# A transformer block on one core: Vector work spread over the beats of a unit, part of it given to GpSimd in another order

## The chip, the cores and the metric

The kernel runs on one core of one Trainium2 chip, in float32, with some matmul operands split into a high and a low part. The metric is the time of one execution in device microseconds (us). Engines are named as in the profile: PE is TensorE (PEld its weight loads), DVE is VectorE ("Vector"), ACT is ScalarE, POOL is GpSimd, SP is the queue that issues nearly all DMAs.

## The reference

A diffusion-transformer block over 16 samples of 256 tokens by 256 channels, 16 heads of 16 channels, with a context of 256 tokens per sample and a condition vector per sample:

```python
shift_a, scale_a, gate_a, shift_m, scale_m, gate_m = split(silu(c) @ W_mod + b_mod, 6)
q, k, v = split((ln(x) * (1 + scale_a) + shift_a) @ W_qkv + b_qkv, 3)       # per head
x = x + gate_a * (softmax(q @ k.T * scale) @ v @ W_proj + b_proj)            # self attention
q_c = ln(x) @ W_qc + b_qc;  k_c, v_c = split(ln(context) @ W_kvc + b_kvc, 2)
x = x + softmax(q_c @ k_c.T * scale) @ v_c @ W_cproj + b_cproj               # cross attention
h = gelu((ln(x) * (1 + scale_m) + shift_m) @ W_mlp1 + b_mlp1)
x = x + gate_m * (h @ W_mlp2 + b_mlp2)                                       # MLP
```

## The kernel before

**Units and beats.** The work is cut into 32 *units*, each the attention of one sample: an s unit is self attention, a c unit cross attention. The order (from line 709) is s0 to s4, then s5, c0, s6, c1 and so on to s15, c10, then c11 to c15. So units 5 to 25 alternate, odd ones s and even ones c, and from unit 26 on all are c. In the loop of line 1123 each unit passes through eight *beats*, `beat(n, k)` (line 981). A beat of unit n does a bit of several units at once: scores of unit n+1, exponentials and value products of unit n, projections and transposes of units n+2 and n+3, layer norms of n+3 and n+4, and the output projection and additions of n-1 to n-3. After the last unit the MLP follows, four chunks per sample.

**Order.** Every engine's instructions run in the order in which the Python code issues them (`InOrder`, line 41): what one waits for holds all behind it on its engine. SP's DMAs stand in one queue of this kind too.

**One beat.** `visit` (line 966) opens it. Four matmuls write scores of unit n+1 into the two PSUM banks `s` (`s_tile`, line 628), and one Vector reduction takes their maxima, `mx`. There is only one such pair of banks, so the next beat's s must wait for this beat's mx. Then four matmuls write the transposed scores of unit n into the pair of banks `st` (`t_part`, line 664), and one ACT activation takes the exponential into `pt` (`exp`); the next st waits for it. After that, even and odd beats differ:

- Even beats do the value products `o` (`av_part`, line 694, 16 matmuls) of one quarter of the heads. In beats 0 and 4 the maxima of half the heads are first transposed (`m_part`, line 656, tile `psm`), scaled by ACT to `m` and sent by DMA into a row of the next q.
- Odd beats run the *lanes* (lines 402 to 431): twelve pairs of 64-row matmuls, each pair for two projections, one with either half of the array. In beat 1 Q with V, in 3 the output projection P with Q, in 5 K with P, in 7 V with K. The first two thirds of a lane read the high part of the input (`xTh`), the last third the low part (`xTl`).

**What the other engines do beside it, before the change.** A projection's K and Q come from PSUM as a high part (ACT, `h_...`) and a low part (DVE, `l_...`, beats 0 and 4) and go by DMA into the stacked tiles `big` for the scores. Layer norms (`layernorm`, line 294): statistics `st` and aggregates `mv` on DVE, an add of epsilon on DVE and a power of -0.5 on POOL for `rs`, then the application `xn` on POOL. Names end with the input: `_s` (x of an s unit), `_c` (context), `_q` (x after self attention, for a c unit), `_m` (MLP). The normed input is transposed on PE into PSUM (`transposed`, line 332, tile `psT`); of an s unit ACT makes the high part and DVE the low part, from the bank; of a c unit ACT makes a high part and a full copy `y` (one buffer), and POOL the low part from these. After attention (`build_post`, line 543) the values `oT` are copied out of PSUM by ACT, pulled by DMA into `U` and, for the denominators, `S`; DVE takes reciprocals of S; these go through DRAM and come back spread as `R`; POOL multiplies U by R; DVE casts U to the high part `xTh_a`, POOL subtracts for the low part `xTl_a`; then come the projection P, and the additions `t`, `x` and the gate `xg` on POOL.

**Where these steps stand in a unit before the change.** Beat 0: transposes of unit n+3, additions of n-3, U of n-2. Beat 1: ACT's high part of the transposes, `xTh_a` (DVE) and `xTl_a` (POOL) of n-2, and the whole layer norm c of unit n+4 (its statistics, aggregates and epsilon on DVE, the rest on POOL). Beat 2: low part or full copy of the transposes; gate. Beat 3: reciprocal. Beat 4: transposes of `xn_q`, copy `oT`, and for an s unit n+4 its statistics, aggregates and epsilon. Beat 5: application of that norm, pull of the first half of oT, R's DMA, statistics of `_q`. Beat 6: full copy `y_q` (ACT), low part `xTl_q` (POOL), then aggregates and epsilon (DVE), power and application (POOL) of `_q`.

**Banks.** PSUM tiles of the short tag `tr` (two banks, `ps_gen`, line 68) hold in turn `psm`, `psT` and `o`; a bank is free again when the last reader of its tile is done. The long tag `gen` (two banks) holds the lanes' results.

Of the kernel before, what the change touches and what calls it, by code (L numbers as in the profile page):

```python
# [21 lines left out]
def pixart_block(  # L22
# [32 lines left out]
    E_ = {'M': ((-17, -12, -10, -1, 1), (0, 3, 4, 7, 9), (8, 11, 13, 15)), 'LN': {'s': 'pool', 'c': 'pool', 'q': 'pool'}, 'ON': (1, 1, 1), 'H': (7, 11, 14, 15), 'AP': 23, 'DV': (0, 1), 'HP': (1, 0), 'W1P': [(-9, 1), (-8, 1), (-7, 1), (-6, 1), (-5, 1), (-5, 5), (-4, 1), (-4, 3), (-4, 5), (-3, 1), (-3, 3), (-3, 5), (-2, 1)], 'W2P': [(-4, 7), (-3, 0), (-3, 4), (-3, 6), (-3, 7), (-2, 2), (-2, 4), (-2, 6), (-1, 0), (-1, 1)], 'PRE': 'z0qp z0kp load rest ld2 one0 silu b12 brow L0a turn L0b b4 L0d scale T0t sc1 hik lok T0h T0l b4 shift b4 hiq L1a L1b bk loq K0a K0b K0x K0yp L1d T1t K0l T1h K0s Q0a Q0m bq Q0h Q0x Q0yp T1l Q0l Q0s z1kp z1qp K1a K1b hiv lov Q1a Q1b K1x K1y K1l K1s Q1x Q1y Q1l Q1s L2a L2b L2c V0a V0b bv b5 ld3', 'SL': {(-1, 0): 'V1a', (-1, 1): 'T2t T2h T2p vone z2kp z2qp', (-1, 2): 'V1b', (-1, 3): 'rest', (-1,4): 'M0 rest one1 ld4', (-1, 5): 'K2a L3a', (-1, 6): 'K2m L3b L3p L3c', (-1, 7): 'd3 one2 rest', (0, 0): 'd6 rest', (0, 1): 'rest', (0, 2): 'd3', (0, 4): 'rest', (1, 0): 'rest', (1, 2): 'rest', (1, 4): 'rest', (30, 0): 'd3', (30, 1): 'd2', (30, 2): 'd3', (30, 5): 'd3', (31, 1): 'd2'}}  # L55
# [45 lines left out]
    def load_x(b):  # L101
        X[b] = work.tile([P, NT, H], F32, tag="x", name=f"x_{b}", bufs=5)
        SP.dma_start(X[b], tok(x, b))
# [84 lines left out]
    def f_load():  # L188
        X[0] = work.tile([P, NT, H], F32, tag="x", name="x_0", bufs=5)
# [104 lines left out]
    def layernorm(src, name):  # L294
# [34 lines left out]
        o.steps, o.pow = [stats, rstd, apply], pow  # L329
# [213 lines left out]
    def build_post(u):  # L543
# [150 lines left out]
    def av_part(u, g):  # L694
# [33 lines left out]
    def mlp_load(b):  # L728
        m = M[b] = Box()
        m.h, m.hT = {}, {}  # L730
        m.xt = work.tile([P, NT, H], F32, tag="x", name=f"x2_{b}", bufs=5)
# [94 lines left out]
    def mlp_w1():  # L826
# [3 lines left out]
        for j in range(4):  # L830
            wf.append(stage(W_mlp1, j * H, f"w1_{j}", "x"))
            yield
# [30 lines left out]
    def mlp_w2():  # L863

        wf = []
        for j in range(4):
            wf.append(work.tile([P, 2, H], F32, tag="x", name=f"w2_{j}", bufs=5))
# [113 lines left out]
    def beat(n, k):  # L981
# [12 lines left out]
        early = lc if lc and lc.b not in (0, B - 1) else None  # L994
        if k == 0 and q2:
# [13 lines left out]
        if k == 0:  # L1009
# [5 lines left out]
            if q3:  # L1015
                q3.T[0].turn()
# [3 lines left out]
            if p3:  # L1020
                p3.add()
            if p2:
                p2.norm()
            if ls and n > 0:
                load(ls)
        elif k == 1:
# [4 lines left out]
            if q3:  # L1031
                q3.T[0].high()
            if p2:
                p2.high()
                p2.low()
            if lc:
                lc.ln[0].steps[0]()
                lc.ln[0].steps[1]()
                lc.ln[0].steps[2]()
        elif k == 2:  # L1040
# [3 lines left out]
            if q3 and q3.kind == "s":  # L1044
                q3.T[0].low()
            elif q3:
                q3.T[0].full()
                q3.T[0].rest_pool()
            if late:
                for f in lx.ln[1].steps:  # L1050
                    f()
            if p1:
                p1.gate()
        elif k == 3:
# [8 lines left out]
            if prev:  # L1063
                p1.recip()
                p1.spread()
        elif k == 4:
# [152 lines left out]
```

## Time and profile before

| | |
|---|---|
| three runs | 810.2, 810.96 and 813.42 us; median 810.96 |
| the profiled execution | 812.03 us, of which the span from first to last instruction is 810.2 |
| granted TensorE clock, mean | 0.982 |
| unit 0 begins its exponentials at | 39.61 us of the span |
| the last of 256 exponentials | unit 31, which begins at 588.19 |
| MLP after the units | to 810.2 us |

A row of the view in order of time gives start, duration, engine, line, operation, output<-inputs with shapes, and in brackets the idle time of the engine before it and what ended it. All instructions have line 51, because a helper issues them; they are told apart by tiles. Merged rows (x2, x4) span from the first start to the last end, and an engine may begin its next instruction some 0.1 us before the end that is written. Rows of groups give count, busy us and mean ns of one, then idle time before them.

### The profile page before, as it was taken

The page shows a single profiled execution, that of the slowest core. Times are in us where ns is not written, and L with a number is a line of the kernel's source. Part 1 is how long each engine was busy: PE and PEld are TensorE (multiplying, and loading weights), DVE is VectorE, ACT ScalarE, POOL GpSimd, SP SyncE. Part 2 cuts the span into 40 slices and gives each one's busy share as a digit, 9 for nine tenths or more (in the row PEclk, how much of TensorE's full clock was granted, in tenths as well). Part 3 has the DMA queues.
Part 4 walks back from the last instruction along what each step waited for, and adds up shares of the span by engine and source line. Part 5 has one row for each costly group of instructions (what it writes and reads, how often), then busy time and mean ns, then how long its engine had stood idle before and what let it go on. Part 6 is the DMA issues. An engine that isn't in the chain of part 4 may idle for free.

```text
span 810.2 us, 22526 instructions
## 1 busy us (share of the span) xinstructions
PE 749.7 (93%) x9071; PEld 616.3 (76%) x9071; DVE 585.7 (72%) x983; ACT 545.3 (67%) x961; POOL 506.1 (62%) x435
## 2 busy tenths in 40 slices
PE   9899889999999999999999787899898899999997
PEld 8677767777777777777777666667568899999997
DVE  4868877878888788887888676777772466566562
ACT  3367767777787877878777666677546466665663
POOL 5754585677656767567676767654546666566563
PEclk9999999999999999999999998999999999999999
DMA  5445334443534545445444434434422222212312
GB/s 193 153 158 187 134 133 154 155 164 137 180 137 164 179 155 167 148 162 180 150 162 165 138 133 157 133 134 168 135 79 73 63 61 78 79 41 78 77 37 58
DMA packets 77165, 106.15 MB, mean 131 GB/s; under 512 B 12355, under 2 KB 40293, under 8 KB 77061
## 3 DMA queue, kind: packets, MB, share of 16 engines
q1 hardware_dynamic: 76084, 103.92, 38.8%
q8 instruction: 71, 1.16, 0.6%
q0 software_dynamic: 160, 0.52, 0.2%
q10 hardware_dynamic: 816, 0.27, 0.1%
q14 instruction: 34, 0.27, 0.1%
HBM read 35.89 MB, written 8.98 MB: 55 GB/s over the span
## 4 chain that ended last, share of the span: by engine, by line
PE 41%; DVE 25%; POOL 18%; issue 9%; ACT 5%; DMA 1%; SPq 0%; POOLq 0%; ACTq 0%; DVEq 0%
DVE mx L51 11%; PE s L51 11%; PE st L51 5%; DVE xn_m L51 5%; PE o L51 5%; POOL x L51 3%; POOL hl L51 3%; PE ps_q L51 3%; PE ph L51 2%; POOL xn_q L51 2%; PE ps_P_c L51 2%; PE ps_k L51 2%; PE ps_P_s L51 2%; PE ps_v_s L51 2%; PE ps_v_c L51 2%
## 5 line engine op out<-in xcount | busy, mean ns | idle before, releaser
L51 DVE TENSOR_REDUCE mx<-s 128x4 f32<-128x1024 f32 x252 | 307.9, 1222 | 97.1 <-PE s L51 95.2
L51 ACT ACTIVATE pt<-st 128x1024 f32<-128x1024 f32 x256 | 261.4, 1021 | 111.6 <-PE st L51 109.9
L51 PE MATMUL s<-big 63*128 63x256 f32 x1008 | 121.8, 314 | 41.4 <-DVE mx L51 38.0
L51 PEld LDWEIGHTS s<-big 63*128 63x128 f32 x1008 | 79.8, 188 | 90.3 <-DVE mx L51 80.7
L51 PE MATMUL o<-pt,v 128*32 128x256 f32 x2048 | 138.0, 387 | 0.0
L51 POOL TENSOR_TENSOR hl<-hf,hh 128x512 fp32r<-128x512 f32 x64 | 89.3, 1405 | 57.6 <-ACT hh L51 47.9
L51 PE MATMUL st<-big 64*128 64x256 f32 (+1 forms) x1040 | 111.3, 287 | 1.7 <-ACT pt L51 1.7
L51 PEld LDWEIGHTS st<-big 64*128 64x128 f32 (+1 forms) x1040 | 84.3, 189 | 6.2 <-ACT pt L51 3.1
L51 PEld LDWEIGHTS o<-pt,v 128*32 128x32 f32 x2048 | 53.7, 109 | 39.0 <-issue 1.3
L51 ACT ACTIVATE hf<-ph,bT 128x256 f32<-128x256 f32 x120 | 50.3, 472 | 28.9 <-PE ph L51 28.9
L51 ACT ACTIVATE hh<-ph,bT 128x256 fp32r<-128x256 f32 x120 | 50.4, 471 | 25.0 <-PE s L51 14.2
L51 PE MATMUL ph<-wkch,wself 128*128 128x256 f32 x256 | 52.8, 289 | 0.0
L51 PE MATMUL ph<-wqch,wself 128*128 128x256 f32 x256 | 51.7, 285 | 0.0
L51 DVE TENSOR_SCALAR xn_m<-x,mv_m,rs_m 128x256 f32<-128x256 f32 x32 | 38.8, 1251 | 10.9 <-POOL rs_m L51 10.9
L51 PE MATMUL s<-big,hh 128*128 128x256 f32 x256 | 46.3, 280 | 0.1
L51 PE MATMUL st<-big,hh 128*128 128x256 f32 x256 | 45.5, 278 | 0.0
L51 POOL TENSOR_TENSOR rs_s<-rs_s,mhalf 128x2 f32<-128x2 f32 x16 | 11.4, 712 | 52.1 <-DVE rs_s L51 50.5
L51 PEld LDWEIGHTS ph<-wkch,wself 128*128 128x128 f32 x256 | 42.7, 195 | 0.3
L51 POOL TENSOR_TENSOR rs_q<-rs_q,mhalf 128x2 f32<-128x2 f32 x16 | 11.4, 712 | 49.4 <-DVE rs_q L51 49.2
L51 PEld LDWEIGHTS ph<-wqch,wself 128*128 128x128 f32 x256 | 42.0, 191 | 0.4 <-DVE hk L51 0.4
L51 POOL TENSOR_TENSOR xTl_q<-y_q,xTh_q 128x512 fp32r<-128x512 f32 x16 | 20.7, 1292 | 34.0 <-ACT y_q L51 28.8
L51 POOL TENSOR_SCALAR xn_c<-c,mv_c,rs_c 128x256 f32<-128x256 f32 x32 | 38.9, 1223 | 1.7
(212 smaller groups left out, 2306.6 us busy)
## 6 DMA issues: line engine op xcount, KB each, us to landing
big<-h_kc SPq DMA_DIRECT2D x32, 256.0 KB
big<-h_qc SPq DMA_DIRECT2D x32, 256.0 KB
big<-h_k SPq DMA_DIRECT2D x31, 256.0 KB
big<-h_q SPq DMA_DIRECT2D x31, 256.0 KB
big<-l_k SPq DMA_DIRECT2D x16, 256.0 KB
big<-l_q SPq DMA_DIRECT2D x16, 256.0 KB
U_s<-oT SPq DMA_DIRECT2D x32, 128.0 KB
g<-gd SPq DMA_DIRECT2D x16, 256.0 KB
```

Source lines behind the costliest of these rows:

```text
L51: i = f(*a, **k)
```

## The change

1. `o_out`, new: the copy of the first half of `oT` moves from beat 4 to beat 5, and its pull from beat 5 to 6.
2. The epsilon add of every layer norm goes from DVE to POOL, just before the power.
3. The cast for `xTh_a` goes from DVE to POOL, and U, cast and `xTl_a` all stand in beat 0.
4. The layer norms are spread: c has statistics in beat 1, the rest in beat 5; an s unit one half of its statistics each in beats 5 and 6 and the rest in beat 7; q has statistics in beat 7 and the rest in beat 1 of the next unit, where before all but the statistics stood behind `xTl_q` in beat 6. (The q norms of the first and last sample, `late`, keep places of their own.)
5. The transposes go from beat 0 to beat 2, their high and low parts or full copy from beats 1 and 2 to beat 3, POOL's `xTl_c` to beat 4.
6. The additions go from beat 0 to beat 2, behind U and its parts; R's DMA is issued last in beat 5.
7. S is laid out as 128x32 in place of 64x64. The tag `x` has six buffers in place of five. One group of three warm-up matmuls (unit 0, beat 2) goes.

The instructions' work is otherwise the same. The core of the diff:

```diff
-            DVE.tensor_scalar(o.rs, o.mv[:, :, 1], EPS, None, ALU.add)
             if power:
                 o.pow()
         def pow():
+            POOL.tensor_scalar(o.rs, o.mv[:, :, 1], EPS, None, ALU.add)
             POOL.tensor_tensor(o.rs, o.rs, mhalf, ALU.pow)
...
+        def stat(t):
+            if t == 0:
+                o.st = work.tile([P, NT, 6], F32, tag="bnst", bufs=4, name=f"st_{name}")
+            DVE.bn_stats(o.st[:, t], src()[:, t])
...
-                o.S = work.tile([64, 64], F32, tag="S", name=f"S_{name}")
-            SP.dma_start(o.S[32 * G:32 * G + 32], u.oT[1:98:32, G])
+                o.S = work.tile([P, 32], F32, tag="S", name=f"S_{name}")
+            SP.dma_start(o.S[64 * G:64 * G + 64], u.oT[1:98:32, G])
...
-            DVE.tensor_copy(aT.xT[0], o.U)
+            POOL.tensor_copy(aT.xT[0], o.U)
...
-        if g % 2 == 1:
-            if g == 1:
+        if g == 3:
+            o_out(u, 1)
+    def o_out(u, half):
+        if True:
+            if half == 0:
                 u.oT = work.tile([P, 2, 2, N], F32, tag="oT", name=f"oT_{u.n}", bufs=1)
-            ACT.copy(u.oT[:, g // 2].rearrange("p g n -> p (g n)"), u.po.rearrange("p g n -> p (g n)"))
+            ACT.copy(u.oT[:, half].rearrange("p g n -> p (g n)"), u.po.rearrange("p g n -> p (g n)"))
...
+        soon = lx if lx and not late else None
...
         if k == 0:
...
-            if q3:
-                q3.T[0].turn()
...
-            if p3:
+            if late and p3:
                 p3.add()
             if p2:
                 p2.norm()
+                p2.high()
+                p2.low()
...
         elif k == 1:
...
-            if q3:
-                q3.T[0].high()
-            if p2:
-                p2.high()
-                p2.low()
             if lc:
                 lc.ln[0].steps[0]()
-                lc.ln[0].steps[1]()
-                lc.ln[0].steps[2]()
+            if soon:
+                soon.ln[1].steps[1]()
+                soon.ln[1].steps[2]()
         elif k == 2:
...
-            if q3 and q3.kind == "s":
-                q3.T[0].low()
-            elif q3:
-                q3.T[0].full()
-                q3.T[0].rest_pool()
+            if q3:
+                q3.T[0].turn()
...
+            if p3 and not late:
+                p3.add()
             if p1:
                 p1.gate()
         elif k == 3:
...
+            if q3:
+                q3.T[0].high()
+                if q3.kind == "s":
+                    q3.T[0].low()
+                else:
+                    q3.T[0].full()
         elif k == 4:
...
-            if lx:
-                lx.T[1].turn()
+            if soon:
+                soon.T[1].turn()
...
+            if q3 and q3.kind == "c":
+                q3.T[0].rest_pool()
...
-            if ls and not late:
-                ls.ln[0].steps[0]()
-                ls.ln[0].steps[1](False)
         elif k == 5:
...
             if cur:
-                cur.post.pull(0)
-            if prev:
-                p1.back()
-            if lx:
-                lx.T[1].high()
-            if ls and late:
-                for f in ls.ln[0].steps:
-                    f()
-            elif ls:
-                ls.ln[0].pow()
-                ls.ln[0].steps[2]()
-            if early:
-                early.ln[1].steps[0]()
+                o_out(cur, 0)
+            if soon:
+                soon.T[1].high()
+            if lc:
+                lc.ln[0].steps[1]()
+                lc.ln[0].steps[2]()
+            if ls:
+                ls.ln[0].stat(0)
...
+            if prev:
+                p1.back()
         elif k == 6:
...
+                cur.post.pull(0)
+            if late:
+                lx.T[1].turn()
-            if lx:
-                lx.T[1].full()
-                lx.T[1].rest_pool()
-            if early:
-                early.ln[1].steps[1]()
-                early.ln[1].steps[2]()
+            if soon:
+                soon.T[1].full()
+                soon.T[1].rest_pool()
+            if ls:
+                ls.ln[0].stat(1)
         elif k == 7:
...
+            if late:
+                lx.T[1].high()
+                lx.T[1].full()
+                lx.T[1].rest_pool()
+            if ls:
+                ls.ln[0].steps[1]()
+                ls.ln[0].steps[2]()
+            if early:
+                early.ln[1].steps[0]()
```

In this code `cur` is unit n, `prev` n-1, `q2`, `q3`, `q4` are units n+2 to n+4, `p1` to `p3` the output work of units n-1 to n-3; `lc` and `ls` are `q4` if it is a c or an s unit, `lx` is `q3` if it is a c unit.

More of the change, by code (lines that the diff above doesn't have):

```diff
@@ L53, in __getattr__ @@
             return issue
[L55 removed]
+    E_ = {'M': ((-17, -12, -10, -1, 1), (0, 3, 4, 7, 9), (8, 11, 13, 15)), 'LN': {'s': 'pool', 'c': 'pool', 'q': 'pool'}, 'ON': (1, 1, 1), 'H': (7, 11, 14, 15), 'AP': 23, 'DV': (0, 1), 'HP': (1, 0), 'W1P': [(-9, 1), (-8, 1), (-7, 1), (-6, 1), (-5, 1), (-5, 5), (-4, 1), (-4, 3), (-4, 5), (-3, 1), (-3, 3), (-3, 5), (-2, 1)], 'W2P': [(-4, 7), (-3, 0), (-3, 4), (-3, 6), (-3, 7), (-2, 2), (-2, 4), (-2, 6), (-1, 0), (-1, 1)], 'PRE': 'z0qp z0kp load rest ld2 one0 silu b12 brow L0a turn L0b b4 L0d scale T0t sc1 hik lok T0h T0l b4 shift b4 hiq L1a L1b bk loq K0a K0b K0x K0yp L1d T1t K0l T1h K0s Q0a Q0m bq Q0h Q0x Q0yp T1l Q0l Q0s z1kp z1qp K1a K1b hiv lov Q1a Q1b K1x K1y K1l K1s Q1x Q1y Q1l Q1s L2a L2b L2c V0a V0b bv b5 ld3', 'SL': {(-1, 0): 'V1a', (-1, 1): 'T2t T2h T2p vone z2kp z2qp', (-1, 2): 'V1b', (-1, 3): 'rest', (-1,4): 'M0 rest one1 ld4', (-1, 5): 'K2a L3a', (-1, 6): 'K2m L3b L3p L3c', (-1, 7): 'd3 one2 rest', (0, 0): 'd6 rest', (0, 1): 'rest', (0, 4): 'rest', (1, 0): 'rest', (1, 2): 'rest', (1, 4): 'rest', (30, 0): 'd3', (30, 1): 'd2', (30, 2): 'd3', (30, 5): 'd3', (31, 1): 'd2'}}
     PE = InOrder(nc.tensor, True)
@@ L101, in load_x @@
     def load_x(b):
-        X[b] = work.tile([P, NT, H], F32, tag="x", name=f"x_{b}", bufs=5)
+        X[b] = work.tile([P, NT, H], F32, tag="x", name=f"x_{b}", bufs=6)
         SP.dma_start(X[b], tok(x, b))
@@ L188, in f_load @@
     def f_load():
-        X[0] = work.tile([P, NT, H], F32, tag="x", name="x_0", bufs=5)
+        X[0] = work.tile([P, NT, H], F32, tag="x", name="x_0", bufs=6)
         ACT.dma_start(X[0], tok(x, 0))
@@ L327, in apply @@
                         ALU.subtract, ALU.mult)
-        o.steps, o.pow = [stats, rstd, apply], pow
+        def stat(t):
+            if t == 0:
+                o.st = work.tile([P, NT, 6], F32, tag="bnst", bufs=4, name=f"st_{name}")
+            DVE.bn_stats(o.st[:, t], src()[:, t])
+        o.steps, o.pow, o.stat = [stats, rstd, apply], pow, stat
         return o
@@ L730, in mlp_load @@
         m.h, m.hT = {}, {}
-        m.xt = work.tile([P, NT, H], F32, tag="x", name=f"x2_{b}", bufs=5)
+        m.xt = work.tile([P, NT, H], F32, tag="x", name=f"x2_{b}", bufs=6)
         SP.dma_start(m.xt, tok(X2d, b))
@@ L830, in mlp_w1 @@
         for j in range(4):
-            wf.append(stage(W_mlp1, j * H, f"w1_{j}", "x"))
+            wf.append(stage(W_mlp1, j * H, f"w1_{j}", "x", 6))
             yield
@@ L866, in mlp_w2 @@
         for j in range(4):
-            wf.append(work.tile([P, 2, H], F32, tag="x", name=f"w2_{j}", bufs=5))
+            wf.append(work.tile([P, 2, H], F32, tag="x", name=f"w2_{j}", bufs=6))
             SP.dma_start(wf[j], W_mlp2[j * H:(j + 1) * H].rearrange("(k p) c -> p k c", p=P))
```

## The prediction

> **What bounds the kernel now.** First the page, its busy shares:
>
> ```profile
> PE 749.7 (93%) x9071; PEld 616.3 (76%) x9071; DVE 585.7 (72%) x983; ACT 545.3 (67%) x961; POOL 506.1 (62%) x435
> ```
>
> No engine is full, but a share is an average over stages. So I cut the span at the exponentials (32 units of eight beats, one `pt` a beat). The view by windows for tile `pt`; length, PE, PEld and ACT with their counts, clock, DMA:
>
> ```profile
> 39.61:182.71 143.10, 33.52 (x504) 13.18 (x508) 65.35 (x64) 0.99 0.45 155
> 182.71:433.95 251.24, 64.23 (x968) 25.04 (x964) 122.58 (x120) 1.00 0.47 161
> 433.95:554.44 120.49, 26.64 (x392) 10.30 (x388) 48.98 (x48) 0.93 0.43 145
> ```
>
> The third count is ACT's exponentials: units 0 to 7 take 17.9 us each, units 8 to 22 take 16.75, units 23 to 28 take 20.1. A unit's own matmuls do not explain the last figure: here lies the largest loss, and the granted clock falls to 0.93. Next I read POOL, DVE and PE in time order inside unit 25:
>
> ```profile
> 470.15 1.29 POOL L51 TENSOR_TENSOR xTl_q<-y_q,xTh_q 128x512 fp32r<-128x512 f32 x1 [5.36 <-ACT y_q L51]
> 471.40 0.71 POOL L51 TENSOR_TENSOR rs_q<-rs_q,mhalf 128x2 f32<-128x2 f32 x1
> 472.21 2.43 POOL L51 TENSOR_SCALAR xn_q<-x,mv_q,rs_q 128x256 f32<-128x256 f32 x2
> 474.61 1.30 POOL L51 TENSOR_TENSOR t_c<-t_c,x 128x512 f32<-128x512 f32 x1
> 475.85 1.30 POOL L51 TENSOR_TENSOR U_s<-U_s,R_s 128x512 f32<-128x512 f32 x1
> ...
> 477.19 0.43 DVE L51 CAST xTh_as<-U_s 128x512 fp32r<-128x512 f32 x1 [1.51 <-POOL U_s L51]
> 478.96 1.21 DVE L51 TENSOR_REDUCE mx<-s 128x4 f32<-128x1024 f32 x1
> ...
> 480.23 0.80 PE L51 MATMUL s<-big 63*128 63x256 f32 x4 [2.68 <-DVE mx L51]
> ```
>
> POOL idles 5.36 us for y_q, then does xTl_q, rs_q, xn_q and t_c before U. Vector's cast waits for U with mx queued behind it, and TensorE's next s waits for mx. POOL is late rather than too slow: its order puts early inputs behind a late one, and U ends 7.0 us after POOL took up y_q (470.15 to 477.15).
>
> In a steady unit the same ring of s and mx (one pair of banks) sets the beat. An even unit (16, a c unit), then five rows of the odd one after it (17):
>
> ```profile
> 315.42 0.46 PE L51 MATMUL s<-big 63*128 63x256 f32 x4
> 316.05 0.28 PE L51 MATMUL psm<-ident,mx 128*16 128x128 f32 x1
> 316.26 1.07 PE L51 MATMUL o<-pt,v 128*32 128x256 f32 x16
> 317.26 0.66 PE L51 MATMUL psT_s<-ident,xn_s 128*128 128x128 f32 x4
> 317.85 0.50 PE L51 MATMUL s<-big 63*128 63x256 f32 x4
> 319.80 0.44 PE L51 MATMUL s<-big 63*128 63x256 f32 x4
> 322.59 0.51 PE L51 MATMUL s<-big 63*128 63x256 f32 x4 [1.11 <-DVE mx L51]
> 324.53 0.48 PE L51 MATMUL s<-big 63*128 63x256 f32 x4
> 326.38 0.50 PE L51 MATMUL s<-big 63*128 63x256 f32 x4
> 328.59 0.45 PE L51 MATMUL s<-big 63*128 63x256 f32 x4
> ...
> 336.70 0.40 PE L51 MATMUL s<-big 63*128 63x256 f32 x4
> 338.42 0.50 PE L51 MATMUL s<-big 63*128 63x256 f32 x4
> 340.38 0.43 PE L51 MATMUL s<-big 63*128 63x256 f32 x4
> 342.77 0.50 PE L51 MATMUL s<-big 63*128 63x256 f32 x4
> 345.13 0.50 PE L51 MATMUL s<-big 63*128 63x256 f32 x4 [0.20 <-DVE mx L51]
> ```
>
> Vector in the even unit:
>
> ```profile
> 319.53 0.42 DVE L51 CAST xTh_ac<-U_c 128x512 fp32r<-128x512 f32 x1
> 320.87 0.54 DVE L51 TENSOR_SCALAR rs_c<-mv_c 128x2 f32<-128x2 f32 x1
> 321.32 1.21 DVE L51 TENSOR_REDUCE mx<-s 128x4 f32<-128x1024 f32 x1
> 322.46 0.86 DVE L51 SCALAR_TENSOR_TENSOR xTl_s<-psT_s,sc,xTh_s 128x256 fp32r<-128x256 f32 x2
> 326.19 0.87 DVE L51 SCALAR_TENSOR_TENSOR l_qc<-ps_qc,bP,h_qc 128x256 fp32r<-128x256 f32 x2
> ```
>
> The even unit's beats 0 to 5 take 2.43, 1.95, 2.79, 1.94, 1.85 and 2.21 us; the odd unit's beats 2 to 5 take 1.72, 1.96, 2.39 and 2.36. The one large wait is in the even beat 2: Vector's cast, c statistics, aggregates and rs, from 319.53 to 321.32, stand ahead of mx. From these rows: s to psm 0.63, psm 0.21, o 1.00, psT 0.59, a lane beat 1.95, mx to the next DVE operation 1.14.
>
> **The change part by part.**
>
> *GpSimd's order.* The chain to P's weights no longer holds Vector: U, the cast and xTl_a stand together at beat 0, the q layer norm at beat 1, adds at beat 2, xTl_c at 4, the c layer norm at 5, xTl_q at 6. The cast's price on POOL is shown at setup, and that of the epsilon add I take from pow of the same shape, 0.71 (the row above); it can lie between 0 and that, below it being cheaper arithmetic on two elements.
>
> ```profile
> L51 POOL CAST wvch<-wvc_f 128x512 fp32r<-128x512 f32 x1 | 0.6, 601 | 0.0
> ```
>
> One late c unit then asks POOL for U 1.25, cast 0.60, low 1.25, two layer norms at 0.71+0.71+2.43, t 1.25, xTl_c and xTl_q 1.29 each: 14.6 us, and 17.1 where an s unit's add and gate (two more at 1.25) fall in. When are the results due? In a unit of 16.9, laid out with the beats below, xn_c starts behind mx of beat 5 and ends at the unit's end, and xTl_q 1.0 into the next. So the cast ends by 2.9 and low by 4.1; the lanes that read them start at about 6.8 and 7.7 (beat 3). xn_q ends by 8.0, its transposes come at 10.3. Only xTl_c in the 17.1 us units is late, by some 0.5. So units 23 to 28 fall to a steady unit's length, 16.9 (below), plus 0.5 in three: 102.9 against 120.5, **-17.6 us**.
>
> Trainium skill, "GPSIMD Engine Reference", section "Engine selection", speaks against this part: elementwise work belongs on VectorE, GpSimd being about half as fast on two inputs, near line rate on one. The rows agree in direction (cast 0.60 against 0.42). By it alone POOL's load would be the bound, which is the first rival.
>
> *Vector and the steady units, beat by beat.* The cast (0.42) and rs (0.54 here) leave DVE; st_c stays in beat 1, mv_c goes to beat 5. Mx of beat 2 is then in time, and beat 2 takes 0.63+1.00+0.59 = 2.2 with the transposes now in it: 2.79 to 2.2, -0.6. Beat 0 loses the transposes, but not all of their 0.59: beats 0 and 1 become like today's 4 and 5 (psm, o, lanes), in which the lanes wait for l_qc (ends 327.06), 4.06 against 4.38 today: -0.3.
>
> The price is in beats 3 to 5. The even unit's xTh_s and xTl_s both move into beat 3, and the odd unit's xTh_c and y_c too. ACT rows:
>
> ```profile
> 319.62 0.83 ACT L51 ACTIVATE xTh_s<-psT_s,sc 128x256 fp32r<-128x256 f32 x2
> 323.44 1.03 ACT L51 ACTIVATE pt<-st 128x1024 f32<-128x1024 f32 x1 [1.55 <-PE st L51]
> 324.75 0.84 ACT L51 ACTIVATE h_qc<-ps_qc,bP 128x256 fp32r<-128x256 f32 x2 [0.29 <-PE ps_qc L51]
> 325.54 0.27 ACT L51 ACTIVATE m<-psm 16x128 fp32r<-16x128 f32 x1
> 325.71 1.00 ACT L51 ACTIVATE pt<-st 128x1024 f32<-128x1024 f32 x1
> 326.62 0.56 ACT L51 COPY oT<-o 128x512 f32<-128x512 f32 x1
> 336.47 0.58 ACT L51 CAST xTh_c<-psT_c 128x512 fp32r<-128x512 f32 x1
> ```
>
> Even unit, s of beat 3 at 0: pt runs 0.85 to 1.88, xTh_s to 2.60, xTl_s (which waits for it; mx is over at 1.7, and the reciprocal fits between) 2.65 to 3.51. Behind it stand mx of beat 4, to 4.65, and psm of beat 4, which in the built order now waits for xTl_s (in the odd unit for y_c), last reader of the bank that it gets: 3.55, not 2.5. Then o to 4.76; pt of beat 4 (0.53 after psm) ends at 5.1; l_qc ends at 5.5, lanes to 6.96. Today these three beats take 6.00: +0.96. Sum for the even unit: -0.3 -0.6 +0.96 = +0.06.
>
> Odd unit: psm waits for y_c (0.85 and 0.92 for pt, 0.50 for xTh_c, 0.58 for y_c: 2.85 instead of 2.5), +0.35 in beat 4; beat 5 falls from 2.36 to 1.95, as the s statistics leave the place ahead of its mx, -0.4; beat 2 rises from 1.72 to 2.2, +0.45; beats 0 and 1 give 0.3 as in the even unit. In beat 6 pt stands behind oT, xTh_q and t_s (0.92+0.52+0.50+0.52 after pt of beat 5 starts), and st of beat 7 waits for it: +0.25. Sum +0.35. So a unit takes about 16.9, even or odd, and units 8 to 22 change by 8 x 0.06 + 7 x 0.35, less rounding: **+2.6 us**. The bounds: no wait left at all, eight product beats of 1.84, eight lane beats of 1.95 and 0.59 three times, 32.1 a pair against 33.5, -10; half a microsecond more in each unit, +8.
>
> *Units 0 to 7.* The transposes of beat 0 waited for xn_s, a warm-up group waited for its bank and goes, and the later units have the POOL chain above in a small form. 143.1 against 7 units at 16.9 and unit 4 at 18.3 (there U stands behind xn_s): 136.6. The 1.4 is cast against need, as above. I take **-5** (-1 to -7), as the first loads stay.
>
> *Small parts.* The prologue's epsilon adds go to POOL at up to 0.71 each, one of them in its chain: +0.5. S as 128x32: half the elements per partition in the reciprocal, twice the pieces in its DMAs; both off the path, 0 (bounds -0.3 to +0.3 a unit, in the range). Six x buffers, the later o copy and pull: hidden, the pull of beat 6 has until the reciprocal of the next beat 3; without that cover a DMA would hold DVE. In the 256 us after unit 28 only that add moves, beside matmuls: 0.
>
> Trainium skill, "TensorE: Matmul & The Clock Gate", section on the HAM clock gate: an idle window of some 3.4 us halves the clock. The trace agrees so far (0.93 around waits such as the 2.68 us one, 1.00 in the steady units). By the rule the full clock comes back with the waits gone, as in the sum; did it stay at 0.93, 7% of 120 us, some 8, would come back.
>
> **Sum:** -17.6 +2.6 -5 +0.5 = -19.5. The profiled execution took 812.0 (span 810.2, 1.8 around it): 792.5. That execution is 1.1 above the median of the three runs, 811.0, so I forecast **791.4**.
>
> **The rivals.** (1) *GpSimd becomes the bound* in units 23 to 28: its 14.6 to 17.1 us per unit leave no room. If waits stretch these six to 18.4, 9 us come back, 1.5 of which are counted: 799. Against it: the slack of 3 to 4 us at U. (2) *Slower:* the bank of beat 4. Each unit's psm waits for the readers of the transposes, and they stand behind pt of beat 3. I price this at 1.0 and 0.35 us; if mx, psm and pt of beat 4 lose another 0.95 together per unit, 25 units cost 24: 815. It decides from about 0.8. Against it: the reader chain is four rows long, each known. (3) *The steady units gain too*, no wait left: -10 in place of +2.6, 779 or less. Against it: the order on ACT and DVE. (4) *The late wait stays*, since U still stands behind xTl_q: 17.6 come back, 809.
>
> **How the numbers follow.** Forecast 0.58; rival 1 0.20; rival 2 0.09; rival 3 0.08; rival 4 0.05. About 0.5% is what a measurement of this kernel can tell from no change. Faster by more: 0.58+0.20+0.08 = 0.86; within: 0.05; slower: 0.09. The range runs from 778 (just below rival 3) to 804 (rival 1 with the steady units' 4 us more).
>
> **What would show it.** Units 23 to 28 near 17 us, no DVE wait for POOL, clock 1.00 there; psm of beat 4 ending a wait for xTl_s or y_c; steady units unchanged in length, their wait moved from beat 2 to beat 4. Wrong, if U still starts over 4 us into a late unit, or if beats 3 to 5 take over 7.5 us.

## The result, and the profile after

The changed kernel takes **797.4 us** (median of four, 796.4 to 799.7) against 810.6 for the kernel before in the same comparison: 0.9835 of it, with a 95% interval of 0.9801 to 0.9868. The forecast was 791.4, with a range of 778 to 804: the time lies in the range, 6.0 us above the forecast. The profiled execution took 799.7 us, with a span of 797.9.

The page of the changed kernel, its busy times and shares: Vector went from 585.7 to 555.5 us, GpSimd from 506.1 to 543.2.

```profile
PE 748.3 (94%) x9065; PEld 611.3 (77%) x9065; DVE 555.5 (70%) x887; ACT 543.4 (68%) x961; POOL 543.2 (68%) x531
```

The view by windows for tile `pt`, cut where the exponentials of units 0, 8, 23 and 29 begin, as before the change (length, PE, PEld and ACT with counts, clock, DMA share, GB/s):

```profile
39.35:175.93 136.58, 33.51 (x504) 13.18 (x508) 65.35 (x64) 1.00 0.48 161
175.93:430.13 254.20, 64.25 (x968) 25.05 (x964) 122.67 (x121) 1.00 0.48 160
430.13:539.91 109.78, 26.71 (x396) 10.27 (x392) 49.04 (x48) 0.98 0.48 159
539.91:797.90 257.99, 13.43 (x204) 5.10 (x196) 24.45 (x24) 0.99 0.26 75
```

Against the same stretches of before, beside the terms of the prediction (us; the prologue is what lies ahead of unit 0's first exponential):

| stretch | before | after | change | predicted |
|---|---|---|---|---|
| prologue | 39.61 | 39.35 | -0.3 | +0.5 |
| units 0 to 7 | 143.10 | 136.58 | -6.5 | -5 |
| units 8 to 22 | 251.24 | 254.20 | +3.0 | +2.6 |
| units 23 to 28 | 120.49 | 109.78 | -10.7 | -17.6 |
| after unit 28 | 255.76 | 257.99 | +2.2 | 0 |
| sum | 810.2 | 797.9 | -12.3 | -19.5 |

So the steady units came out as worked out, and the miss lies in units 23 to 28, with a smaller one behind them. One by one they take 16.90, 22.11, 16.91, 17.79, 16.90 and 19.17 us: the odd ones are steady units now, the even ones are not. R's DMA for unit 24 on SP, then GpSimd in the first part of this unit, whose exponentials begin at 447.03, in order of time:

```profile
442.52 0.66 SPq L51 DMA_DIRECT2D R_c<-rd_c  x1
445.43 1.29 POOL L51 TENSOR_TENSOR xTl_q<-y_q,xTh_q 128x512 fp32r<-128x512 f32 x1
450.31 1.29 POOL L51 TENSOR_TENSOR U_c<-U_c,R_c 128x512 f32<-128x512 f32 x1 [3.59 <-DMA R_c<-rd_c]
451.66 0.61 POOL L51 CAST xTh_ac<-U_c 128x512 fp32r<-128x512 f32 x1
452.36 1.29 POOL L51 TENSOR_TENSOR xTl_ac<-U_c,xTh_ac 128x512 fp32r<-128x512 f32 x1
453.74 0.23 POOL L51 TENSOR_SCALAR rs_q<-mv_q 128x2 f32<-128x2 f32 x1
454.05 0.72 POOL L51 TENSOR_TENSOR rs_q<-rs_q,mhalf 128x2 f32<-128x2 f32 x1
454.88 2.44 POOL L51 TENSOR_SCALAR xn_q<-x,mv_q,rs_q 128x256 f32<-128x256 f32 x2
457.28 1.28 POOL L51 TENSOR_TENSOR t_s<-t_s,g 128x512 f32<-128x512 f32 x1
458.64 1.28 POOL L51 TENSOR_TENSOR x<-xg,t_s 128x512 f32<-128x512 f32 x1
459.88 1.26 POOL L51 TENSOR_TENSOR xg<-x,g 128x512 f32<-128x512 f32 x1
461.10 1.26 POOL L51 TENSOR_TENSOR xTl_c<-y_c,xTh_c 128x512 fp32r<-128x512 f32 x1
```

and TensorE behind it:

```profile
457.37 0.55 PE L51 MATMUL psT_q<-ident,xn_q 128*128 128x128 f32 x3 [0.83 <-POOL xn_q L51]
462.42 0.38 PE L51 MATMUL ps_kc<-xTl_c,wkch 64*128 64x256 f32 x1 [2.88 <-POOL xTl_c L51]
```

The new order works as meant, U stands right behind xTl_q; but R is not there until 450.31, 7.8 us after SP issued its DMA. From then on GpSimd has no gap for 12 us, and the last of the row, xTl_c, holds the K lanes of beat 5. GpSimd is not late by its order any more; it is late because its work is dense between two dates, the landing of R and the start of the lanes that read xTl_c. Beats 4 and 5 of this unit take 2.98 and 5.71 us.

In the steady units the predicted wait is there, psm of beat 4 for the last reader of the transposes' bank. Waits of units 8 to 22 (us in total, times, longest):

```profile
PEld s L51 <- DVE mx L51: 17.9, 38, 0.6
PE psm L51 <- DVE xTl_s L51: 8.7, 8, 1.1
PEld psm L51 <- ACT y_c L51: 3.2, 7, 0.5
```

Unit 18 shows it once, beats 2 to 4, rows of ACT, DVE and PE in order of time:

```profile
349.08 1.02 ACT L51 ACTIVATE pt<-st 128x1024 f32<-128x1024 f32 x1
351.34 1.03 ACT L51 ACTIVATE pt<-st 128x1024 f32<-128x1024 f32 x1 [1.24 <-PE st L51]
352.26 0.83 ACT L51 ACTIVATE xTh_s<-psT_s,sc 128x256 fp32r<-128x256 f32 x2
353.20 0.88 DVE L51 SCALAR_TENSOR_TENSOR xTl_s<-psT_s,sc,xTh_s 128x256 fp32r<-128x256 f32 x2 [0.67 <-ACT xTh_s L51]
354.22 0.27 PE L51 MATMUL psm<-ident,mx 128*16 128x128 f32 x1 [1.09 <-DVE xTl_s L51]
354.75 1.00 ACT L51 ACTIVATE pt<-st 128x1024 f32<-128x1024 f32 x1
```

From pt to pt, beat 2 takes 2.26 and beat 3 takes 3.41 us. The eight beats of unit 18 take 1.65, 2.01, 2.26, 3.41, 1.66, 1.89, 1.83, 2.26.

### The profile page after: what moved, and what is told of

Read it like the earlier page. It is cut to its first block, busy times and chain, and to the rows that moved or that the text cites. A ratio compares the mean times of both kernels' runs of the same rounds, so it can differ in the third digit from the quotient of the medians.

```text
span 797.9 us, 22671 instructions
## 1 busy us (share of the span) xinstructions
PE 748.3 (94%) x9065; PEld 611.3 (77%) x9065; DVE 555.5 (70%) x887; ACT 543.4 (68%) x961; POOL 543.2 (68%) x531
## 4 chain that ended last, share of the span: by engine, by line
PE 48%; DVE 19%; POOL 15%; ACT 10%; issue 5%; DMA 1%; SPq 0%; POOLq 0%; ACTq 0%; DVEq 0%
PE s L51 10%; PE o L51 10%; DVE mx L51 8%; PE st L51 6%; DVE xn_m L51 4%; POOL hl L51 3%; POOL x L51 3%; PE ps_k L51 2%; PE ps_q L51 2%; PE ps_qc L51 2%; PE ps_v_s L51 2%; PE ps_kc L51 2%; POOL rs_m L51 2%; DVE xTf_m L51 2%; PE psm L51 2%
## 5 line engine op out<-in xcount | busy, mean ns | idle before, releaser
L51 PE MATMUL s<-big 63*128 63x256 f32 x1008 | 119.4, 308 | 5.4 <-DVE mx L51 3.0
L51 PE MATMUL st<-big 64*128 64x256 f32 (+1 forms) x1040 | 114.9, 292 | 2.6 <-ACT pt L51 1.5
L51 POOL TENSOR_SCALAR xn_q<-x,mv_q,rs_q 128x256 f32<-128x256 f32 x32 | 39.0, 1229 | 1.7
L51 PEld LDWEIGHTS s<-big,hh 128*128 128x128 f32 x256 | 39.5, 192 | 0.3 <-ACT hh L51 0.3
```

The costliest lines, as they stand in the source:

```text
L51: i = f(*a, **k)
```

## The experiments

Times are medians, with the ratio to the kernel before of the same runs (810.2 to 811.2); the stretches are cut in each profile as above.

| run | us | ratio, 95% | units 0-7 | 8-22 | 23-28 |
|---|---|---|---|---|---|
| changed kernel | 797.4 | 0.980 to 0.987 | 136.6 | 254.2 | 109.8 |
| the same once more | 797.5 | 0.979 to 0.991 | 136.6 | 254.0 | 107.8 |
| R ahead of the load | 794.2 | 0.977 to 0.988 | 136.6 | 254.1 | 104.9 |
| that once more, one execution | 792.8 | | 136.6 | 254.1 | 104.9 |
| xTh in beat 2 | 784.4 | 0.965 to 0.972 | 133.1 | 245.3 | 105.2 |
| GpSimd's order alone | 794.4 | 0.975 to 0.986 | 137.0 | 245.7 | 107.0 |
| adds behind xTl_c | 794.1 | 0.976 to 0.991 | 136.7 | 254.1 | 103.8 |
| three edits together, xTl_s first | 779.3 | 0.957 to 0.963 | 132.8 | 245.3 | 102.2 |
| and the MLP's add on Vector | **776.9** | 0.957 to 0.962 | 132.8 | 245.4 | 102.2 |
| the cast alone back on Vector | 812.3 | 0.997 to 1.003 | 143.8 | 262.2 | 108.8 |
| the rest alone, q norm in beat 7 | 892.4 | 1.094 to 1.103 | 157.8 | 308.1 | 127.0 |
| the rest alone, q norm in beats 5 and 6 | 875.9 | 1.078 to 1.084 | 155.3 | 296.4 | 126.7 |

### Why units 24 and 26 stay long: R, or GpSimd's load

First R, put back ahead of the context load:

```diff
             if cur:
                 o_out(cur, 0)
+            if prev:
+                p1.back()
...
                 load(v)
-            if prev:
-                p1.back()
```

> The changed kernel with one part undone: R's DMA goes back ahead of the context load in beat 5. Theory A (units 23 to 28 missed their forecast because R lands late: POOL waited 3.59 us for it in unit 24, behind 256 KB of context load): R is issued 0.6 us sooner and 0.9 us less of bytes stand before it, so U starts 1 to 1.5 us sooner in unit 24 and about 1 us sooner in unit 30; unit 24 falls from 22.1 to about 20.8, the whole to about 795. If R landed 4.3 us after its issue as it does in the steady s units, unit 24 would fall by 3.6 or more and the whole to 793. Theory B (POOL's 17.1 us of work in units 24 and 26 is the bound, whatever R does): unit 24 stays at 22, the whole at 797.4.

Unit 24 takes 17.51 and unit 26 takes 17.46; U of unit 24 starts 4.9 us after R's issue (441.92), with next to no wait:

```profile
446.79 1.29 POOL L51 TENSOR_TENSOR U_c<-U_c,R_c 128x512 f32<-128x512 f32 x1
```

That is theory A with R nearly as early as in the s units. But how steady is the landing? First the changed kernel once more, then this one:

> The changed kernel as it is, once more. Is unit 24's 22.1 us the same in each execution? Theory V (R's landing varies from one execution to the next, 5 to 8 us after the issue, and POOL's full load turns each us of it into one of unit 24): unit 24 anywhere from 18.5 to 22, units 26 and 28 again at 17.8 and 19.2, the whole 795 to 800. Rival (a fixed queue position gives a fixed landing): unit 24 at 22.1 again.

> R ahead of the context load once more, for a second look at R's landing in unit 24: theory V without a part for the place gives anything from 5 to 8 us after the issue and unit 24 at 18 to 22; if the place in the queue decides, 4.9 again and unit 24 at 17.5.

In the second execution of the changed kernel unit 24 takes 18.00, within theory V; unit 26 takes 19.89, where 17.8 was expected. U's rows there are

```profile
446.84 1.28 POOL L51 TENSOR_TENSOR U_c<-U_c,R_c 128x512 f32<-128x512 f32 x1 [0.76 <-DMA R_c<-rd_c]
482.25 1.29 POOL L51 TENSOR_TENSOR U_c<-U_c,R_c 128x512 f32<-128x512 f32 x1 [1.25 <-PE o L51]
```

So the landing varies with the same program. In the five profiles of this study that have R behind the load and GpSimd waiting for it in unit 24, U starts 7.8, 5.0, 6.3, 5.2 and 5.5 us after R's issue. In the four with R ahead of the load (the two runs above and the last two kernels below) it starts 4.8 to 5.0 us after the issue and waits 0.2 at most. So a start much later than 5 us was seen only with R behind the load; that the place in the queue alone decides it is not shown, since behind the load it was 5.0 once too. (Ahead of U in unit 26 the view names a product of PE; U does not read that one, and with R ahead of the load the wait is gone, so I take it for R's.) With 3.59, 0.76 and at most 0.2 us of wait ahead of U, unit 24 takes 22.11, 18.00 and 17.51. The first of these holds a loss of clock as well, and so does the 19.89 of unit 26 (see the clock in the next section). Without the wait 0.6 us are left above 16.9.

That remainder and the price of the wait are GpSimd's load, by the run that leaves R where the change put it and moves 3.8 us of adds out of the way:

```diff
         elif k == 2:
...
+            heavy = soon and cur.kind == "c" and p3 and unit(n - 3).kind == "s"
-            if p3 and not late:
+            if p3 and not late and not heavy:
                 p3.add()
-            if p1:
+            if p1 and not heavy:
                 p1.gate()
...
         elif k == 4:
...
             if q3 and q3.kind == "c":
                 q3.T[0].rest_pool()
+            if soon and cur.kind == "c" and p3 and unit(n - 3).kind == "s":
+                p3.add()
+                if p1:
+                    p1.gate()
```

> The changed kernel; in units 24 and 26 alone GpSimd's two s adds and the gate (3.8 us) stand behind xTl_c in place of ahead of it. Theory B (POOL's load puts xTl_c late): unit 24 falls from 22.1 by 3.5 to 4.5, unit 26 from 17.8 to 16.9, the whole to about 792. Theory A (R's landing alone): unit 26 falls by 0.9, unit 24 by 1 or less, the whole to about 796.

GpSimd in its unit 24:

```profile
449.46 1.29 POOL L51 TENSOR_TENSOR U_c<-U_c,R_c 128x512 f32<-128x512 f32 x1 [2.10 <-DMA R_c<-rd_c]
450.82 0.61 POOL L51 CAST xTh_ac<-U_c 128x512 fp32r<-128x512 f32 x1
...
456.43 1.29 POOL L51 TENSOR_TENSOR xTl_c<-y_c,xTh_c 128x512 fp32r<-128x512 f32 x1
457.66 1.30 POOL L51 TENSOR_TENSOR t_s<-t_s,g 128x512 f32<-128x512 f32 x1
```

R comes 2.10 us late and nothing happens: units 24 and 26 take 16.92 each. Theory B of this run holds, though not in the strong form of the first (the bound whatever R does). It takes both: the adds ahead of xTl_c made the row dense, and a late R then passed straight to the lanes. Each of the two edits is within the spread of the changed kernel's own times (794 against 797, intervals that overlap); the unit lengths, not the medians, carry this verdict.

### The bank of beat 4

```diff
         elif k == 2:
...
             if q3:
                 q3.T[0].turn()
+                q3.T[0].high()
...
         elif k == 3:
...
             if q3:
-                q3.T[0].high()
                 if q3.kind == "s":
                     q3.T[0].low()
```

> The changed kernel with ScalarE's first copy of the turned tile (xTh) issued in beat 2, right behind the transposes, in place of beat 3 behind that beat's exponential. Theory C (the prediction's beats 3 to 5: psm of beat 4 waits for the last reader of the transposes' bank, xTl_s in even units, y_c in odd ones): beat 3 falls from 3.41 to about 2.3 in even units and from 2.75 to about 2.2 in odd ones, beats 2 and 4 stay; some 12 even units by 1.1 and 13 odd ones by 0.5 make -19, so about 778. Rival D: the wait only moves, ScalarE then waits for the transposes ahead of the exponential of beat 3, and units keep 16.9 us: 795 to 798.

784.4 us, so theory C, at two thirds of the expected size (13 us less than the changed kernel, where 19 were expected). Its unit 16, beats 2 to 4:

```profile
307.72 1.02 ACT L51 ACTIVATE pt<-st 128x1024 f32<-128x1024 f32 x1
309.24 0.84 ACT L51 ACTIVATE xTh_s<-psT_s,sc 128x256 fp32r<-128x256 f32 x2 [0.50 <-PE psT_s L51]
309.98 1.03 ACT L51 ACTIVATE pt<-st 128x1024 f32<-128x1024 f32 x1
311.09 0.77 DVE L51 SCALAR_TENSOR_TENSOR xTl_s<-psT_s,sc,xTh_s 128x256 fp32r<-128x256 f32 x2
312.01 0.27 PE L51 MATMUL psm<-ident,mx 128*16 128x128 f32 x1 [0.23 <-DVE xTl_s L51]
```

ACT waits 0.50 for the transposes, at a time when it had idled for the next st anyway, and pt follows without loss. Psm waits 0.23 instead of 1.09; beat 3 falls from 3.41 to 2.55. In odd units beat 3 falls from 2.75 to 2.27, while beat 4 grows from 1.94 to 2.09: 16.60 instead of 16.91. Beat 3 of the even unit does not reach 2.3; the reciprocal, 0.34, stands ahead of xTl_s on Vector there. The run with all edits, below, turns these two around.

### The two halves of the change

GpSimd's order alone, in the kernel before:

```diff
-            DVE.tensor_copy(aT.xT[0], o.U)
+            POOL.tensor_copy(aT.xT[0], o.U)
...
         if k == 0:
...
-            if p3:
+            if late and p3:
                 p3.add()
             if p2:
                 p2.norm()
+                p2.high()
+                p2.low()
...
         elif k == 1:
...
-            if p2:
-                p2.high()
-                p2.low()
+            if soon:
+                soon.ln[1].pow()
+                soon.ln[1].steps[2]()
...
         elif k == 2:
...
+            if p3 and not late:
+                p3.add()
...
         elif k == 6:
...
-                early.ln[1].steps[1]()
-                early.ln[1].steps[2]()
+                early.ln[1].steps[1](False)
```

> The kernel before with GpSimd's part of the change alone: U, the cast (now on GpSimd) and xTl_a together in beat 0, the q layer norm's power and scaling in the next beat 1, the adds in beat 2. Vector's statistics, the transposes, R, the store and the loads stay as before. Theory A': GpSimd's order carries the gain of units 23 to 28 (prediction: 120.5 to 103), and Vector's beat 2 loses the cast's 0.42 in units 8 to 22: 10 to 17 us in units 23 to 28 and 3 to 6 before them, 788 to 797 in all. Rival E: the late units gain from the spread of Vector's work and of the transposes, not from GpSimd's order: units 23 to 28 stay over 115, the whole over 803.

794.4, theory A'; ahead of unit 23 it gains 11.7 us, more than the 3 to 6 expected. The windows of its profile:

```profile
38.90:175.92 137.02, 33.51 (x504) 13.18 (x508) 65.42 (x64) 1.00 0.48 162
175.92:421.57 245.65, 64.24 (x968) 25.04 (x964) 122.73 (x120) 1.00 0.49 164
421.57:528.59 107.02, 25.69 (x392) 10.01 (x388) 49.05 (x48) 1.00 0.49 163
528.59:795.90 267.31, 13.60 (x208) 5.19 (x200) 24.44 (x24) 0.99 0.25 72
```

Up to the end of unit 28 the order alone gains 25.9 us (554.4 to 528.6), the whole change 14.5 (to 539.9). So the rest of the change, added to it, cost 11.3, most of it in the steady units (245.7 to 254.2), where the wait of beat 4 is new. (The last stretch is another matter, see the end.)

The rest alone is the changed kernel with the same edits taken back. It was run with the q layer norm whole in beat 7, and then with it in beats 5 and 6 as in the kernel before:

> The changed kernel with GpSimd's order and the cast undone: adds and U in beat 0, the cast on Vector and xTl_a in beat 1, the q layer norm whole in beat 7. Transposes, the other layer norms, statistics, R, o copy, pull and loads stay as changed. It is the complement of the order alone. Theory A' (the order carries the gain, the moved transposes cost): units 8 to 22 at 254 or more, units 23 to 28 at 116 to 122, the whole 808 to 820. Rival E (the spread of Vector's work carries a good part): units 23 to 28 under 113, the whole under 803.

> The rest of the change alone once more (GpSimd's order and the cast undone), with the q layer norm in beats 5 and 6 as before instead of whole in beat 7. Theory F (in the first version of the rest alone, the q layer norm in beat 7 held U back, and Vector's cast with it): units 8 to 22 at 254 to 262, the whole 810 to 825. Theory G (the cast on Vector waits in any case, since the c layer norm, moved to beat 5, puts 3.4 us more of GpSimd's work between mv_c and U): units 8 to 22 over 270, the whole over 830.

In the first run neither theory came near, 892 us; in the second, 876, theory G holds. The waits of units 8 to 22 there:

```profile
DVE xTh_ac L51 <- POOL U_c L51: 31.8, 8, 4.0
DVE xTh_as L51 <- POOL U_s L51: 16.4, 7, 2.5
```

Every unit waits now, 2.3 or 4.0 us, not only the late ones: the layer norms that the change moved to beats 5 and 7 lie on GpSimd ahead of U, and the adds with them, and Vector's cast waits behind all of it. So the halves do not add: -25.9 alone, +63.7 alone (q in beats 5 and 6), -14.5 together, up to unit 28. Which part of the order makes the rest bearable, the cast's engine or U's place? The cast taken back to Vector, in beat 1 as before, with xTl_a, which reads it, behind it:

```diff
-            POOL.tensor_copy(aT.xT[0], o.U)
+            DVE.tensor_copy(aT.xT[0], o.U)
...
         if k == 0:
...
                 p2.norm()
-                p2.high()
-                p2.low()
...
         elif k == 1:
...
+            if p2:
+                p2.high()
+                p2.low()
             if lc:
                 lc.ln[0].steps[0]()
```

> The changed kernel with the cast alone taken back: U and the adds keep their new places on GpSimd, the cast stands on Vector in beat 1, behind that beat's maxima, and xTl_a follows it. It parts the two things that the rest alone took back at once. Theory H (the cast on Vector is what holds the units): in steady even units U stands behind xn_s and ends 3.9 us after the unit's first exponential; the cast waits for it 1.5 us, the c statistics and the maxima of beat 2 come 1.6 us later. Odd units, whose U ends ahead of the unit's start, lose nothing. Some 10 even units by 1.6: units 8 to 22 at 266, the whole 810 to 816. Theory I (the place of U and of the adds is what counts): units 8 to 22 at 254 to 257, the whole 797 to 801.

812.3, theory H, with a smaller price in units 8 to 22 than I gave (262.2, not 266): the even beat 2 grows from 2.26 to 3.34. The cast's waits in units 8 to 22, and the cast of unit 16:

```profile
DVE xTh_ac L51 <- POOL U_c L51: 11.1, 8, 1.4
```

```profile
327.09 0.43 DVE L51 CAST xTh_ac<-U_c 128x512 fp32r<-128x512 f32 x1 [1.41 <-POOL U_c L51]
```

One cast of 0.43 us, on the engine that must not wait, takes back as much as the whole change gained (1.000 of before, 0.997 to 1.003): 7.2 us in units 0 to 7, 8.0 in units 8 to 22. Units 23 to 28 keep their gain, 108.8; in units 23 to 27 the cast waits for U 0.22 us at most.

### Together

The three edits, and xTl_s ahead of the reciprocal in beat 3:

> The changed kernel with three edits at once: R ahead of the context load, xTh in beat 2, the s adds and the gate of units 24 and 26 behind xTl_c; besides, Vector's xTl_s stands ahead of the reciprocal in beat 3 (psm of beat 4 still waited 0.23 us for xTl_s in an even unit). Theory (three separate waits): against xTh in beat 2 alone, units 24 and 26 fall from 18.1 to 16.6, -3.0, the even units by 0.25 each, -2.5, R's late landing about -0.5: 778 to 780. Rival (the edits overlap, only the largest counts): 783 to 785.

779.3, in the expected range, but not by the expected terms. Units 24 and 26 do fall from 18.1 to 16.60, -3.0. The even units, which were to gain 0.25 each from the reciprocal's new place, stay at 16.14: beat 3 falls from 2.56 to 2.39, and beat 5 rises from 1.89 to 2.10. So the units explain 3.3 of the 5.1 us between the medians (up to the end of unit 28 the profiles take 519.8 and 523.5 us, and the prologue makes 0.4 of that), and the agreement of the whole is in part luck. Odd units take 16.6; unit 28 stays at 19.17. Then the last term, the epsilon add of the MLP's layer norms:

```diff
-            POOL.tensor_scalar(o.rs, o.mv[:, :, 1], EPS, None, ALU.add)
+            (DVE if name[0] == "m" else POOL).tensor_scalar(o.rs, o.mv[:, :, 1], EPS, None, ALU.add)
```

> The three edits together, and the epsilon add of the MLP's layer norms back on Vector (those of the units stay on GpSimd). Theory M: in the MLP the chain aggregates, add, power, scaling is on the path, and GpSimd's add with its handover costs 0.12 us a sample (the stores of the output stand 12.02 us apart before and 12.14 after): spacing 12.02 again, 11 samples by 0.12 make -1.3 against the three edits, 778. Rival N (the spacing comes from something else, as the x buffers): 12.14 and the same time, 779.3.

776.9, the fastest kernel of the study, 0.9593 of before (0.9567 to 0.9619). In the MLP the add stood on the path; the chain that ended last, of the changed kernel, has it between Vector's aggregates and GpSimd's power:

```profile
743.32 0.23 DVE mv_m L51 x2
743.54 0.08 issue
743.62 0.22 POOL rs_m L51
...
743.92 0.72 POOL rs_m L51
```

The output's stores show the spacing of the samples, of the changed kernel first and then of this one:

```profile
691.58 0.38 SPq L51 DMA_DIRECT2D out_dram<-y  x1
703.72 0.38 SPq L51 DMA_DIRECT2D out_dram<-y  x1
```

```profile
693.37 0.38 SPq L51 DMA_DIRECT2D out_dram<-y  x1
705.40 0.38 SPq L51 DMA_DIRECT2D out_dram<-y  x1
```

12.14 and 12.03 us, theory M. The spacing is 12.02 before the change too, and 12.12 to 12.15 in all ten profiles with the add on GpSimd (GpSimd's order alone is a case of its own, see the end). By the spacing alone this is worth 11 x 0.12 = 1.3 us; the difference of the medians is 2.4, and no run explains the rest.

## Why the prediction was right or wrong

**The steady units: right in the mechanism and in the sum.** The even unit's beats 3 to 5 were worked out as 6.96 and take 3.41 + 1.66 + 1.89 = 6.96. The odd unit was to grow by 0.35 and grows by 0.3; the stretch was given +2.6 (its own terms, 8 x 0.06 + 7 x 0.35, make 2.9) and grew by 3.0. Single beats are off. In the odd unit the wait falls into beat 3 and not 4, as counted from pt to pt, beat 5 gave 0.07 instead of 0.4, and the 0.25 for the wait of st did not come. In the even unit beats 0 and 1 gave 0.6 instead of 0.3, and beat 2 gave 0.3 instead of 0.6. These errors cancel, so the close agreement of the sum is partly luck.

**The term that missed: "Only xTl_c in the 17.1 us units is late, by some 0.5. So units 23 to 28 fall to a steady unit's length, 16.9 (below), plus 0.5 in three: 102.9".** It is the term of -17.6, measured -10.7. Of the 6.9 us, 4.7 are unit 24 (22.11 against 17.4), 0.4 unit 26, 1.8 unit 28. The mechanism was right (GpSimd's order; alone it gains 13.5 in these units), and so was the name of the late tile. Where R is early even the size holds: with R ahead of the load units 24 and 26 are 0.6 longer than 16.9. What failed is that the list of due times took R for granted. The prediction has no sentence on R's new place, though the change moves it, and counted on 3 to 4 us of slack at U. GpSimd's wait of 3.59 us for R used it up, and the row behind U, filled without a gap by the q layer norm, the additions and the gate, carried the delay on to xTl_c. So the first rival, GpSimd as the bound, is half right: its load costs 0.6 us in each of two units where R is early, and more only with a late R. That rival's 799 lies closer to the measured time than the forecast does, and its 110.4 for these units (six of 18.4) lies next to the measured 109.8, but by two long units, of which one has another reason, and not by six equal ones. Of the signs that were to show the prediction wrong, U starts 3.3 us into unit 24 and not over 4, but beats 3 to 5 of this unit take 11.4 us, where the limit was 7.5.

**Unit 28** was given 17.4 and takes 19.17, and 19.14 to 19.19 in every run with the rest of the change. It was 18.73 before, the shortest of the long even units. Its beat 1 (3.20 us, 3.09 before) holds a setup projection of the MLP (`ps_cpm`, 1.04 us of matmul), and beats 3 to 5 a cut of W1 on Vector and GpSimd; that is work which the trace of before shows. Its beats 6 and 7 take 2.26 and 2.75, against 1.77 and 2.31 before: the last q norm's transposes and copies, which stood in beats 4 to 6, now stand there (the `late` branch of the change). The prediction counts neither; no run takes one of them away.

**Units 0 to 7:** worked out as -6.5, taken as -5, measured -6.5. The equality is partly luck: unit 4 takes 17.04 and not 18.3, while unit 3, which the sum puts at 16.9, stays at 17.99 (17.92 before).

**After unit 28:** given 0, measured +2.2. The epsilon add "beside matmuls" is on the MLP's path: 1.3. Unit 30 took 17.91 against 17.07, and here the wait for R counts one for one: in the changed kernel's two profiles, the two with R ahead of the load, xTh in beat 2, the adds behind xTl_c and the three edits, GpSimd waits 4.33 to 5.09 us for R ahead of U in unit 30, and the unit's length, 17.15 to 17.91, is this wait plus 12.82 or 12.83 each time. In all seven R stands at the same place of SP's queue there, behind a load of MLP weights, and U starts 4.7 to 5.5 us after its issue (4.4 before the change). Why it varies stays open.

**The epsilon add** was taken at 0.71, "between 0 and that", and takes 0.23; the cast was taken at 0.60 and takes 0.61. The prologue's +0.5 did not come (-0.3).

**The clock** is 1.00 in units 23 to 28 where their waits are gone (adds behind xTl_c, the three edits), 0.98 in the changed kernel, 0.92 and 0.93 in the two runs of the rest alone. A wait can cost twice: the time itself, and then slower matmuls. Behind its wait of 2.88 us unit 24 has 0.66 in beat 6, which takes 2.47 us instead of 1.77. In the second execution TensorE waits 1.65 us for xTl_c in unit 26, and then beats 6 and 7 take 1.4 us longer than in the first (wait 0.98, clock 1.00). Beat 6 of the two units, of the changed kernel first and then of its second execution (length, PE with its count, clock, DMA share, GB/s):

```profile
464.40:466.87 2.47, 2.47 (x28) 0.66 0.00 0
```

```profile
495.71:498.50 2.79, 2.79 (x28) 0.51 0.42 102
```

In units 8 to 28 of all thirteen profiles, each single wait of TensorE of 2.88 us or more was followed by a clock of 0.50, none of up to 1.63 us was, and of the fourteen between (1.65 to 2.76 us) four were. What decides between these is not shown. The Trainium skill, "TensorE: Matmul & The Clock Gate", section on the HAM clock gate, as cited in the prediction, agrees in direction.

**Trainium skill, "GPSIMD Engine Reference", "Engine selection"**, which keeps elementwise work off GpSimd: the rows keep agreeing on the price of one instruction (cast 0.61 against 0.43 on Vector), and the MLP's add is a case for the rule. For the cast of U it is the other way round: 0.43 us on Vector with its wait against 0.61 on GpSimd makes 812 against 797 us.

## What to carry to other kernels

When an engine's queue is reordered, give each instruction two dates, when its input is there and when its result is due, and add up the work between the two: an engine that is 68% busy was the bound for 12 us because one input came late into a dense row. List the DMAs that feed that row with their landing times, and how these vary from execution to execution, before calling a slack free. And a cheap instruction on a slower engine is free only where nobody waits for it: the epsilon add of 0.23 us shows in the MLP, where the next step waits for it, as 0.12 us a sample more than on Vector.

## What was not expected of the hardware

A DMA of 256 KB (R, from DRAM to 128 partitions) ended GpSimd's wait for it 7.8 and 5.0 us after its issue at the same place of the same program, in two executions whose DMA engines were equally busy in the 2 us behind the issue (0.91 and 0.95). What makes the difference of 2.8 stays open.

An add of 128x2 on Vector has two prices. Of the 64 epsilon adds of before, 46 take 0.17 us. The other 18 take 0.52 to 1.09: these are the ones that run beside a two-input GpSimd subtraction (`xTl_a`, in two cases `xTl_c`), and no add of 0.17 has any GpSimd instruction beside it. The 0.54 of `rs_c` that the prediction took off Vector's beat 2 was one of the 18, so most of it was this overlap.

The MLP has two courses. In the profile of GpSimd's order alone, whose MLP code is that of before, the output's stores stand 12.90 us apart instead of 12.02, all through the stage, at a granted clock of 1.00:

```profile
697.78 0.38 SPq L51 DMA_DIRECT2D out_dram<-y  x1
710.68 0.38 SPq L51 DMA_DIRECT2D out_dram<-y  x1
```

Over eleven spacings this makes 9.7 of the 11.5 us by which its last stretch (267.3) exceeds that of before (255.8). Its four times fall into two pairs, 797.7 and 798.5, 789.4 and 791.2, which fits; so its median says less than its stretches do. What chooses the course was not tried. The changed kernel's second series, R ahead of the load and the adds behind xTl_c each have one time 8 to 10 us above their median (805.0, 802.5 and 803.7); that this is the same course is a guess, as no trace shows these executions.
